# The compact form of the reflections as a stream of its own among the blocks of 16, with other clocks in the planner

## The chip, the cores and the metric

The kernel runs on one core of a Trainium2 chip. The metric is the time of one execution on the device, in microseconds (us); lower is better.

## What is computed

Two layers of a graph network on `x` of 64 x 256 x 256 with one 256 x 256 adjacency matrix `adj`, all in fp32:

```python
# layer 0
h = relu(layernorm(x));  G = adj * adj
h = relu(G @ (h @ W1)); h = relu(G @ (h @ W2)); x = x + G @ (h @ W3)
# layer 1
h = relu(layernorm(x))
deg = sum(adj, 0) + sum(adj, 1) - diag(adj); d = rsqrt(deg)
_, U = eigh(d[:, None] * (diag(deg) - adj) * d[None, :])
h = relu((U.T @ h) @ W1 + b1)
x = x + U @ (h @ W2 + b2)
```

Layer 0 is many matrix products (TensorE). The eigenvectors `U` are one long chain of small, dependent steps, most of them on VectorE. Layer 1 needs both.

## The kernel before, in words

**The chain** (class `Eigen`). `tridiagonalize` (line 393) brings the 256 x 256 matrix to tridiagonal form in 254 steps. In step k, a row `xr` and a column `xc` hold the row and column to be cleared. ScalarE squares and sums the row into `tail` (line 431), VectorE forms `xa` (437), `nn` (440), then through a square root on ScalarE `nb` (450) and `ac` (453). TensorE turns `ac` into a row (`pu`, tile psB, line 454); from it VectorE makes `uau` (465), `c` (467), the row `wr` (469) and the next row `xn` (474, 475), and then, off the shortest way to the next step, the next column (478, 479) and the two updates of the matrix per half (482, 483). The matrix is held as two halves of 128 rows; the first 127 steps work on both, the others on one. The rows get shorter with k: 256 - (k + 1) columns. The vectors of the reflections are kept in `us` (tile q2) and their factors in `gams` (tile z2).

`leaves` (861) then solves 16 blocks of 16 at once. Its core, `all_parts` (721), is 32 sweeps; in each, 15 pairs of a reciprocal and a scalar_tensor_tensor on one column follow one another, and the turning of the vectors of the sweep before lies between them. Its work space is tile q1. At its end it turns its results into matrix form through TensorE (psB, psC) and makes `dc`, the column of eigenvalues. Then `reflections` (502) makes one 256 x 256 matrix `QT` of all 254 reflections: two products of `us`, seven doubling steps (two mask products on VectorE, two products on TensorE, a copy on ScalarE, four products, two subtractions on VectorE from PSUM tile psD), and closing products. `level` (1182) runs for 32, 64, 128 and 256 and merges pairs of blocks; its first TensorE work is to turn `dc` and `zc` into rows (line 1235). `QT` is needed only behind the last level, for `u` and `ut`. After that a flag is computed and read, and a branch (`mend`, 1625) is passed.

**The streams** (class `Layers`). Layer 0 goes over 32 pairs of matrices. `products` (1743) and `rows` (1769) are generators that yield one operation at a time: matrix products with their copies out of PSUM, and norms with loads and stores. `last` adds the result to `x` on VectorE (128x512 from PSUM), `norm1`, `turn_rows` and `for_layer1` make `hw`, the rows that layer 1 begins with. `layer1` (1963) follows when streams and chain are done.

**The order of work.** TensorE and ScalarE execute in exactly the order in which the program issues; VectorE, GpSimd and SyncE are ordered by the compiler's scheduler. `Pace` (143) decides how chain and streams interleave: it keeps a clock for each engine and a time for each tile's content, from costs in `Op` (80): `busy`, for which an engine is taken, and `until`, when a result can be used. Before each chain operation on TensorE it issues stream operations that by its clocks can start before the chain's is ready plus `LATER`; it does so before operations of other engines too. Chain costs are multiplied by `SLOWER`, in the blocks by `IN_BLOCKS`. VectorE's clock may lag behind a waiting operation by `WINDOW` (1.0 us), for the scheduler's freedom. All these operations are recorded on line 188 (`issue`), so that the profile tells them apart by tiles. The costs and the factor of the tie between them are:

```python
    each = 6.3 if self.name == "reciprocal" else 2.0 if self.name == "tensor_tensor_scan" else 1.0
    self.busy = 0.065 + each * n / 960 + 0.08 * sums
    self.until = self.busy + (0.18 if self.name == "scalar_tensor_tensor" else 0.13)
...
    start = max(start, clock[engine])
    clock[engine] = max(clock[engine] + busy, start + busy - self.WINDOW)
```

For TensorE, `busy` is 0.165 for a transpose and the larger of 0.22 and 4 x columns / 2400 for a product.

Of the kernel before, what the change touches and what calls it, by code (L numbers as in the profile page):

```python
# [23 lines left out]
OP = mybir.AluOpType  # L24
# [3 lines left out]
N = 256  # L28
P = 128
H = 2  # L30
# [49 lines left out]
class Op:  # L80


    def __init__(self, part, call, args, kwargs):
        self.engine, self.call, self.args, self.kwargs = ENGINES[part], call, args, kwargs
        self.name = call.__name__
        free = lambda a: int(np.prod([int(n) for n in a.shape[1:]]))
        named = dict(kwargs)
        outs = [named.pop("out")] if "out" in named else [args[0]]
        ins = [a for a in [*(args if "out" in kwargs else args[1:]), *named.values()] if isinstance(a, bass.AP)]
        total = named.pop("accum_out", None)  # L90
        if isinstance(total, bass.AP):
            outs.append(total)
            ins = [a for a in ins if a is not total]
        self.outs, self.ins = [span(a) for a in outs], [span(a) for a in ins]
        n = max(free(a) for a in outs[:1] + ins) if self.engine == "DVE" else free(outs[0])
        sums = len(outs) > 1

        if self.engine == "PE":
            self.busy = 0.165 if "transpose" in self.name else max(4 * n / 2400, 0.22)
            self.until = self.busy + 0.35  # L100
        elif self.engine == "ACT":
            pointers = any(isinstance(kwargs.get(k), bass.AP) for k in ("scale", "bias"))
            self.busy = 0.13 + n / 1400 + 0.12 * pointers + 0.19 * sums
            self.until = self.busy + 0.12
        elif self.engine == "DVE":
            each = 6.3 if self.name == "reciprocal" else 2.0 if self.name == "tensor_tensor_scan" else 1.0
            self.busy = 0.065 + each * n / 960 + 0.08 * sums
            self.until = self.busy + (0.18 if self.name == "scalar_tensor_tensor" else 0.13)
        elif self.engine == "POOL":
            self.busy = 0.2 + 2 * n / 960  # L110
            self.until = self.busy + 0.1
        else:
            self.busy, self.until = 0.1, 4.0


def span(a):

    step = a.ap[0][0]
    lo = a.offset % step if step else a.offset
    return a.tensor.name, lo, lo + sum((int(n) - 1) * abs(int(s)) for s, n in a.ap[1:]) + 1  # L120
# [22 lines left out]
class Pace:  # L143
# [2 lines left out]


    WINDOW = 1.0
    SLOWER, IN_BLOCKS = 1.025, 1.07
    LATER = {"PE": 0.15, "ACT": 0.1}  # L150

    def __init__(self, nc):
        self.slower = self.SLOWER
# [36 lines left out]
    def chain(self, op):  # L190
        if not self.on:
            return op.call(*op.args, **op.kwargs)
        late = self.LATER.get(op.engine, 0.0)
        self.run(self.ready(op) + late, "ACT" if op.engine == "ACT" else None)
        return self.issue(op, self.slower)

    def run(self, limit, whole=None):

        while True:
            first, stream = limit, None  # L200
            for x in self.streams * 2:
                op = x.head()
                if op is not None:
                    start = max(self.ready(op), self.clock[op.engine]) + op.busy * (op.engine == whole)
                    if start < first:
                        first, stream = start, x
            if stream is None:
                return
            self.issue(stream.op)
            stream.op = None  # L210

    def finish(self):
        self.run(float("inf"))
        assert not any(x.more for x in self.streams)
        self.streams, self.on = (), False
# [21 lines left out]
class Eigen:  # L237
# [264 lines left out]
    def reflections(self, us, gams):  # L502


        nc = self.nc
        half = lambda tag: self.mat(tag).rearrange("p h n -> p (h n)")[:, 0 : H * P].rearrange("p (h n) -> p h n", h=H)
        tri = self.mat("m1").rearrange("p h n -> p (h n)")
        tri2 = self.mat("m2").rearrange("p h n -> p (h n)")
        steps = 7
        mask = [(tri if i < 4 else tri2)[:, i % 4 * P : (i % 4 + 1) * P] for i in range(steps)]  # L510
        for i in range(steps):
            nc.sync.dma_start(out=mask[i], in_=self.ap["c_tri"][i])
        s = self.mat("m3")
        self.product(s, us, us, "psD")
        vt = self.mat("m4")
        self.copy_out(vt, self.transpose(us, "psC"))
        t, tt, low, x = half("bs"), half("rb"), half("mask"), half("notm")
        for h in range(H):
            self.tt(t[:, h, :], self.ident[:, 0, 0:P], gams[:, h * P : (h + 1) * P], OP.mult)
        nc.scalar.copy(tt, t)  # L520
        flat2 = lambda v: v.rearrange("p h n -> p (h n)")
        for i in range(steps):
            for h in range(H):
                self.tt(low[:, h, :], s[:, h, h * P : (h + 1) * P], mask[i], OP.mult)
            ps = self.psum("psD")
            for h in range(H):
                at = slice(h * P, (h + 1) * P)
                nc.tensor.matmul(ps[:, at], lhsT=low[:, h, :], rhs=t[:, h, :], start=True, stop=True)
            nc.scalar.copy(flat2(x), ps[:, 0:N])
            ps = self.psum("psD")  # L530
            for h in range(H):
                at, to = slice(h * P, (h + 1) * P), slice(N + h * P, N + (h + 1) * P)
                nc.tensor.matmul(ps[:, at], lhsT=tt[:, h, :], rhs=x[:, h, :], start=True, stop=True)
                nc.tensor.matmul(ps[:, to], lhsT=x[:, h, :], rhs=tt[:, h, :], start=True, stop=True)
            self.tt(flat2(t), flat2(t), ps[:, 0:N], OP.subtract)
            self.tt(flat2(tt), flat2(tt), ps[:, N : 2 * N], OP.subtract)

        g = self.mat("q1")
        ps = self.psum("psD")
        for h in range(H):  # L540
            nc.tensor.matmul(ps[:, h * N : (h + 1) * N], lhsT=t[:, h, :], rhs=vt[:, h, :], start=True, stop=True)
        self.copy_out(g, ps)
        ps = self.psum("psD")
        nc.tensor.matmul(ps[:, 0:N], lhsT=s[:, 0, P:N], rhs=g[:, 0, :], start=True, stop=True)
        nc.scalar.copy(low.rearrange("p h n -> p (h n)"), ps[:, 0:N])
        ps = self.psum("psD")
        nc.tensor.matmul(
            ps[:, 0:N], lhsT=t[:, 1, :], rhs=low.rearrange("p h n -> p (h n)"), start=True, stop=True
        )
        self.tt(g[:, 1, :], g[:, 1, :], ps[:, 0:N], OP.subtract)  # L550
        qt = self.mat("QT")
        ps = self.psum("psD")
        for m in range(H):
            for h in range(H):
                nc.tensor.matmul(
                    ps[:, m * N : (m + 1) * N],
                    lhsT=vt[:, h, m * P : (m + 1) * P],
                    rhs=g[:, h, :],
                    start=h == 0,
                    stop=h == H - 1,  # L560
                )
        self.tt(
            qt.rearrange("p h n -> p (h n)"), self.ident.rearrange("p h n -> p (h n)"), ps, OP.subtract
        )
        return qt


    def scale_and_cut(self, d, e):
# [1041 lines left out]
    def join(self, u, ut, bad, reflections=None):  # L1610
        d = self.row("DV")
        self.nc.vector.tensor_copy(d, self.d)
        self.pace.slower = self.pace.IN_BLOCKS
        zt, dc = self.leaves(d, self.e, bad)
        self.pace.slower = self.pace.SLOWER
        if reflections is not None:
            self.qt = self.reflections(*reflections)
        for n in LEVELS:
            dc = self.level(n, zt, dc, self.rho, self.sg, bad)
        z = self.mat("m0")  # L1620
        self.copy_out(z, self.transpose(zt))
        self.product(u, self.qt, z)
        self.product(ut, z, self.qt)
# [422 lines left out]
```

## Time and profile before

| what | before |
|---|---|
| median of 3 runs (lowest to highest) | 2575.08 us (2575.02 to 2576.18) |
| the profiled execution's own time | 2575.78 us |
| its span, first to last instruction | 2573.6 us |
| mean granted clock of TensorE | 0.991 |
| tridiagonalization, two halves / one half | 22.9 to 836 / 836 to 1467 us |
| blocks of 16 | 1467 to 1893 us |
| reflections | 1893 to 1938 us |
| levels, u and ut | 1938 to 2397 us |
| layer 1 | 2403 to 2574 us |

The first page gives each engine's busy time and the span in 40 slices, a digit for each slice's busy tenths. PE is TensorE's products, PEld its weight loads, DVE VectorE, ACT ScalarE, POOL GpSimd, SP SyncE. An fp32 product shows as two records, and the ends of TensorE's records are modelled, so that a busy TensorE isn't at its peak; start to start is the safer reading. A row of waits names who waited, for whom, the sum in us, how often, and the longest. A row of the timeline gives start, length, engine, line, operation, tiles (out<-in, buffer numbers left out: `m` stands for tiles m0 to m4, `q` for q1 and q2), shape and count, and in brackets the idle time of the engine before it with what ended it. The chain of waits follows the end of the execution back through what released each step.

### The profile page before, as it was taken

What the parts mean: (1) busy time and instruction counts of PE and PEld (TensorE: products, weight loads), DVE (VectorE), ACT (ScalarE), POOL (GpSimd) and SP (SyncE); (2) the same over time, 40 slices, a digit from 0 to 9 for tenths busy, and PEclk for the clock granted to TensorE, in tenths of its full rate; (3) what the DMA queues carried; (4) which work ended last, traced back from release to release, by engine and by line L of the source; (5) the groups of instructions that cost most, each with busy time, mean ns of one, the idle gap of its engine ahead of it and who ended that gap; (6) DMA issues with size and microseconds to landing.
All of it is one profiled execution on the core that took longest, in us unless ns stands there. A gap on an engine that the chain in (4) does not pass through costs nothing. (4 is left out here: it accounts for less than half of the span.)

```text
span 2573.6 us, 38875 instructions
## 1 busy us (share of the span) xinstructions
PE 2414.5 (94%) x8986; PEld 1554.1 (60%) x8986; DVE 2237.4 (87%) x13785; ACT 1027.5 (40%) x3080; POOL 469.7 (18%) x2006
## 2 busy tenths in 40 slices
PE   7888888888899999999999999999999999999899
PEld 3555455545555566666666666565666666565788
DVE  8999999999999999999999999999958898788343
ACT  4234433443344444444444443333433344343322
POOL 1222222222222222223322100000000000000343
PEclk9999999999999999999999999999999999999899
DMA  3000000000000000000000000000000000000576
GB/s 114 17 5 21 17 21 5 21 17 21 5 21 18 21 22 21 22 21 22 22 15 12 22 21 22 21 21 17 21 21 25 9 21 21 21 21 1 171 252 208
DMA packets 59406, 90.06 MB, mean 35 GB/s; under 512 B 5793, under 2 KB 42785, under 8 KB 59169
## 3 DMA queue, kind: packets, MB, share of 16 engines
q1 hardware_dynamic: 59168, 87.52, 10.2%
q8 instruction: 73, 1.20, 0.2%
q14 instruction: 165, 1.34, 0.2%
HBM read 47.13 MB, written 40.37 MB: 34 GB/s over the span
## 5 line engine op out<-in xcount | busy, mean ns | idle before, releaser
L188 PE MATMUL bank<-y,L_gnn_W 128*128 128x512 f32 x2048 | 908.2, 595 | 0.0
L188 PEld LDWEIGHTS bank<-y,L_gnn_W 128*128 128x128 f32 x2048 | 381.3, 191 | 432.3 <-issue 415.1
L188 PE MATMUL bank<-L_gnn_W,s 128*128 128x256 f32 x2048 | 463.8, 380 | 2.5 <-ACT s L188 2.5
L188 PEld LDWEIGHTS bank<-L_gnn_W,s 128*128 128x128 f32 x2048 | 383.4, 191 | 52.9 <-ACT s L188 3.7
L188 ACT ACTIVATE s<-bank 128x512 f32<-128x512 f32 x384 | 223.1, 585 | 153.0 <-PE bank L188 152.2
L188 PE MATMUL bank<-gt,s 128*128 128x256 f32 x1024 | 236.4, 384 | 6.5 <-ACT s L188 6.4
L188 PE MATMUL bank<-L_gnn_W,y 128*128 128x512 f32 x512 | 229.2, 593 | 2.1 <-ACT p L188 2.1
L188 PEld LDWEIGHTS bank<-gt,s 128*128 128x128 f32 x1024 | 193.3, 193 | 42.3 <-ACT s L188 10.3
L188 ACT ACTIVATE junk<-xr 128x254 f32<-128x254 f32 (+63 forms) x254 | 78.0, 307 | 339.6 <-DVE xr L188 333.7
L188 POOL COPY alpha<-xr 128x1 f32<-128x1 f32 x254 | 97.0, 382 | 556.7 <-DVE xr L188 539.1
L1936 POOL TENSOR_TENSOR xb<-x,ub 128x512 f32<-128x512 f32 x64 | 79.8, 1270 | 590.0 <-DVE ub L1902 517.0
L188 PE MATMUL psB<-ident,ac 128*128 128x128 f32 x381 | 86.7, 282 | 105.1 <-DVE ac L188 100.5
L188 ACT COPY y<-bank 128x512 f32<-128x512 f32 x192 | 110.9, 582 | 150.6 <-PE bank L188 150.2
L188 PEld LDWEIGHTS psB<-ident,ac 128*128 128x128 f32 x381 | 42.1, 136 | 212.1 <-issue 148.2
L188 ACT ACTIVATE h<-x,shift,scale 128x256 f32<-128x256 f32 x256 | 136.5, 589 | 66.9 <-DVE shift L188 65.0
L188 PEld LDWEIGHTS bank<-L_gnn_W,y 128*128 128x128 f32 x512 | 95.2, 190 | 101.2 <-issue 89.0
L188 ACT ACTIVATE junk<-x 128x256 f32<-128x256 f32 x256 | 105.6, 412 | 90.0 <-DVE x L188 74.8
L188 ACT ACTIVATE junk<-x,nm 128x256 f32<-128x256 f32 x256 | 129.0, 504 | 27.8 <-DVE nm L188 23.6
L188 DVE SCALAR_TENSOR_TENSOR A<-wr,uc,A 128x255 f32<-128x255 f32 (+63 forms) x381 | 139.6, 367 | 0.0
L188 POOL TENSOR_TENSOR e<-nb,alpha 128x1 f32<-128x1 f32 x254 | 48.1, 189 | 458.7 <-DVE nb L188 449.9
L188 DVE SCALAR_TENSOR_TENSOR q<-q 128x1 f32<-128x1 f32 (+1 forms) x576 | 120.1, 209 | 11.9 <-ACT q L188 1.0
L188 DVE SCALAR_TENSOR_TENSOR A<-xr,wc,A 128x255 f32<-128x255 f32 (+63 forms) x381 | 129.4, 364 | 0.0
(597 smaller groups left out, 4472.2 us busy)
## 6 DMA issues: line engine op xcount, KB each, us to landing
x<-x SPq DMA_DIRECT2D x60, 512.0 KB, 3.4
x<-in_x_dram SPq DMA_DIRECT2D x64, 256.0 KB, 3.6
out_dram<-out SPq DMA_DIRECT2D x64, 256.0 KB, 2.2
hw<-hw SPq DMA_DIRECT2D x60, 256.0 KB, 2.7
L_gnn_W<-in_L_gnn_W_dram SPq DMA_DIRECT2D x1, 2048.0 KB, 11.0
L_gnn_W<-in_L_gnn_W_dram SPq DMA_DIRECT2D x1, 1024.0 KB, 13.6
L_gnn_W<-in_L_gnn_W_dram SPq DMA_DIRECT2D x1, 512.0 KB, 6.4
mask<-in_c_blk_dram SPq DMA_DIRECT2D x2, 256.0 KB, 2.8
```

Of the source, the lines that this page charges most:

```text
L188: return op.call(*op.args, **op.kwargs)
L1936: nc.gpsimd.tensor_tensor(xb[:, :, b, :], x1[:, :, b, :], self.ub2, OP.add)
```

## The change

`reflections` becomes a generator: each instruction that it issued is yielded instead, with the same shapes and in the same order. `join` wraps it in a `Stream`, puts it ahead of the two of layer 0 while `leaves` runs, and issues whatever is left of it by the new `Pace.complete` before the first level. Its matrix `g` goes from tile q1, which `all_parts` uses, to q2. The costs of VectorE in `Op` get a term of 0.06 us for scalar_tensor_tensor and for operations with an operand of one column; the extra time until a result can be used is 0.125 us for all. `SLOWER`, `IN_BLOCKS` and `LATER` for TensorE get other values.

```diff
@@ Op
-            self.busy = 0.065 + each * n / 960 + 0.08 * sums
-            self.until = self.busy + (0.18 if self.name == "scalar_tensor_tensor" else 0.13)
+            pointers = self.name == "scalar_tensor_tensor" or any(a.shape[1:] == [1] for a in ins[1:])
+            self.busy = 0.065 + 0.06 * pointers + each * n / 960 + 0.08 * sums
+            self.until = self.busy + 0.125
@@ Pace
-    SLOWER, IN_BLOCKS = 1.025, 1.07
-    LATER = {"PE": 0.15, "ACT": 0.1}
+    SLOWER, IN_BLOCKS = 1.03, 1.11
+    LATER = {"PE": 0.1, "ACT": 0.1}
+    def complete(self, stream):
+        while stream.more:
+            if stream.head() is not None:
+                self.issue(stream.op)
+                stream.op = None
@@ reflections
-        nc = self.nc
+        nc = self.pace.later
-            nc.sync.dma_start(out=mask[i], in_=self.ap["c_tri"][i])
+            yield nc.sync.dma_start(out=mask[i], in_=self.ap["c_tri"][i])
...
-                self.tt(low[:, h, :], s[:, h, h * P : (h + 1) * P], mask[i], OP.mult)
+                yield nc.vector.tensor_tensor(low[:, h, :], s[:, h, h * P : (h + 1) * P], mask[i], OP.mult)
...
-            self.tt(flat2(t), flat2(t), ps[:, 0:N], OP.subtract)
-            self.tt(flat2(tt), flat2(tt), ps[:, N : 2 * N], OP.subtract)
-        g = self.mat("q1")
+            yield nc.vector.tensor_tensor(flat2(t), flat2(t), ps[:, 0:N], OP.subtract)
+            yield nc.vector.tensor_tensor(flat2(tt), flat2(tt), ps[:, N : 2 * N], OP.subtract)
+        g = self.mat("q2")
...
-        qt = self.mat("QT")
+        self.qt = qt = self.mat("QT")
...
-        return qt
@@ join
         self.pace.slower = self.pace.IN_BLOCKS
+        if reflections is not None:
+            reflections = Stream(self.reflections(*reflections))
+            self.pace.streams = reflections, *self.pace.streams
         zt, dc = self.leaves(d, self.e, bad)
+        if reflections is not None:
+            self.pace.complete(reflections)
         self.pace.slower = self.pace.SLOWER
-        if reflections is not None:
-            self.qt = self.reflections(*reflections)
         for n in LEVELS:
```

More of the change, by code (lines that the diff above doesn't have):

```diff
@@ L511, in reflections @@
         for i in range(steps):
-            nc.sync.dma_start(out=mask[i], in_=self.ap["c_tri"][i])
+            yield nc.sync.dma_start(out=mask[i], in_=self.ap["c_tri"][i])
         s = self.mat("m3")
-        self.product(s, us, us, "psD")
-        vt = self.mat("m4")
-        self.copy_out(vt, self.transpose(us, "psC"))
+        flat2 = lambda v: v.rearrange("p h n -> p (h n)")
+        ps = self.psum("psD")
+        for m in range(H):
+            for h in range(H):
+                yield nc.tensor.matmul(
+                    ps[:, m * N : (m + 1) * N],
+                    lhsT=us[:, h, m * P : (m + 1) * P],
+                    rhs=us[:, h, :],
+                    start=h == 0,
+                    stop=h == H - 1,
+                )
+        yield nc.scalar.copy(flat2(s), ps)
+        vt = self.mat("m4")
+        ps = self.psum("psC")
+        for a in range(H):
+            for b in range(H):
+                yield nc.tensor.transpose(
+                    ps[:, a * N + b * P : a * N + (b + 1) * P],
+                    us[:, b, a * P : (a + 1) * P],
+                    self.ident[:, 0, 0:P],
+                )
+        yield nc.scalar.copy(flat2(vt), ps)
         t, tt, low, x = half("bs"), half("rb"), half("mask"), half("notm")
         for h in range(H):
-            self.tt(t[:, h, :], self.ident[:, 0, 0:P], gams[:, h * P : (h + 1) * P], OP.mult)
-        nc.scalar.copy(tt, t)
-        flat2 = lambda v: v.rearrange("p h n -> p (h n)")
+            yield nc.vector.tensor_tensor(t[:, h, :], self.ident[:, 0, 0:P], gams[:, h * P : (h + 1) * P], OP.mult)
+        yield nc.scalar.copy(tt, t)
         for i in range(steps):
             for h in range(H):
-                self.tt(low[:, h, :], s[:, h, h * P : (h + 1) * P], mask[i], OP.mult)
+                yield nc.vector.tensor_tensor(low[:, h, :], s[:, h, h * P : (h + 1) * P], mask[i], OP.mult)
             ps = self.psum("psD")
@@ L527, in reflections @@
                 at = slice(h * P, (h + 1) * P)
-                nc.tensor.matmul(ps[:, at], lhsT=low[:, h, :], rhs=t[:, h, :], start=True, stop=True)
-            nc.scalar.copy(flat2(x), ps[:, 0:N])
+                yield nc.tensor.matmul(ps[:, at], lhsT=low[:, h, :], rhs=t[:, h, :], start=True, stop=True)
+            yield nc.scalar.copy(flat2(x), ps[:, 0:N])
             ps = self.psum("psD")
@@ L532, in reflections @@
                 at, to = slice(h * P, (h + 1) * P), slice(N + h * P, N + (h + 1) * P)
-                nc.tensor.matmul(ps[:, at], lhsT=tt[:, h, :], rhs=x[:, h, :], start=True, stop=True)
-                nc.tensor.matmul(ps[:, to], lhsT=x[:, h, :], rhs=tt[:, h, :], start=True, stop=True)
-            self.tt(flat2(t), flat2(t), ps[:, 0:N], OP.subtract)
-            self.tt(flat2(tt), flat2(tt), ps[:, N : 2 * N], OP.subtract)
-        g = self.mat("q1")
+                yield nc.tensor.matmul(ps[:, at], lhsT=tt[:, h, :], rhs=x[:, h, :], start=True, stop=True)
+                yield nc.tensor.matmul(ps[:, to], lhsT=x[:, h, :], rhs=tt[:, h, :], start=True, stop=True)
+            yield nc.vector.tensor_tensor(flat2(t), flat2(t), ps[:, 0:N], OP.subtract)
+            yield nc.vector.tensor_tensor(flat2(tt), flat2(tt), ps[:, N : 2 * N], OP.subtract)
+        g = self.mat("q2")
         ps = self.psum("psD")
         for h in range(H):
-            nc.tensor.matmul(ps[:, h * N : (h + 1) * N], lhsT=t[:, h, :], rhs=vt[:, h, :], start=True, stop=True)
-        self.copy_out(g, ps)
+            yield nc.tensor.matmul(ps[:, h * N : (h + 1) * N], lhsT=t[:, h, :], rhs=vt[:, h, :], start=True, stop=True)
+        yield nc.scalar.copy(flat2(g), ps)
         ps = self.psum("psD")
-        nc.tensor.matmul(ps[:, 0:N], lhsT=s[:, 0, P:N], rhs=g[:, 0, :], start=True, stop=True)
-        nc.scalar.copy(low.rearrange("p h n -> p (h n)"), ps[:, 0:N])
+        yield nc.tensor.matmul(ps[:, 0:N], lhsT=s[:, 0, P:N], rhs=g[:, 0, :], start=True, stop=True)
+        yield nc.scalar.copy(low.rearrange("p h n -> p (h n)"), ps[:, 0:N])
         ps = self.psum("psD")
-        nc.tensor.matmul(
+        yield nc.tensor.matmul(
             ps[:, 0:N], lhsT=t[:, 1, :], rhs=low.rearrange("p h n -> p (h n)"), start=True, stop=True
         )
-        self.tt(g[:, 1, :], g[:, 1, :], ps[:, 0:N], OP.subtract)
-        qt = self.mat("QT")
+        yield nc.vector.tensor_tensor(g[:, 1, :], g[:, 1, :], ps[:, 0:N], OP.subtract)
+        self.qt = qt = self.mat("QT")
         ps = self.psum("psD")
@@ L554, in reflections @@
             for h in range(H):
-                nc.tensor.matmul(
+                yield nc.tensor.matmul(
                     ps[:, m * N : (m + 1) * N],
@@ L561, in reflections @@
                 )
-        self.tt(
+        yield nc.vector.tensor_tensor(
             qt.rearrange("p h n -> p (h n)"), self.ident.rearrange("p h n -> p (h n)"), ps, OP.subtract
         )
-        return qt
     def scale_and_cut(self, d, e):
```

## The prediction

> **What bounds the kernel now.** I read the totals and slices of the page, then stretches, waits, the rows around the moved step, and last the chain of waits.
>
> ```profile
> PE 2414.5 (94%) x8986; PEld 1554.1 (60%) x8986; DVE 2237.4 (87%) x13785; ACT 1027.5 (40%) x3080; POOL 469.7 (18%) x2006
> ...
> PE   7888888888899999999999999999999999999899
> ...
> DVE  8999999999999999999999999999958898788343
> ```
>
> Two engines look full. The stretches are tridiagonalization with two row halves, with one half, blocks of 16, reflections, levels, layer 1 (columns: stretch, length, busy time and count of PE, PEld, DVE, ACT, POOL):
>
> ```profile
> 22.90:836.00 813.10, 713.69 (x2670) 435.89 (x2669) 778.97 (x4508) 316.93 (x997) 200.32 (x868) 0.99 0.05 16
> 836.00:1466.70 630.70, 625.04 (x2328) 395.41 (x2328) 586.21 (x4209) 294.25 (x974) 180.62 (x1032) 1.00 0.06 20
> 1466.70:1893.20 426.50, 407.47 (x1380) 252.46 (x1379) 391.32 (x3038) 161.99 (x465) 7.18 (x33) 0.98 0.06 19
> 1893.20:1937.80 44.60, 44.52 (x193) 29.37 (x193) 14.81 (x53) 21.49 (x62) 0.00 (x0) 1.00 0.10 30
> 1937.80:2397.40 459.60, 445.78 (x1613) 287.01 (x1612) 385.90 (x1806) 180.55 (x484) 0.00 (x0) 0.98 0.05 16
> 2403.40:2573.60 170.20, 166.16 (x768) 145.74 (x768) 66.96 (x99) 38.89 (x64) 79.85 (x64) 1.00 0.72 238
> ```
>
> TensorE idles 99 us in the first stretch, 19 in the blocks, 14 in the levels, hardly elsewhere. VectorE is at 92 to 96% until the blocks end and at 33% (14.8 of 44.6 us) in the reflections. The first idle time has one owner, the transposes of line 454, of 0.55 to 0.96 us in the mean per step:
>
> ```profile
> PE psB L188 <- DVE ac L188: 100.5, 126, 2.6
> ```
>
> There the eigen chain sets the pace and TensorE comes too early. The reflections stand alone in the chain (start, length, row, wait before it):
>
> ```profile
> 1894.44 0.08 DVE L188 DVE_READ_ACCUMULATOR junk<-DV,ident 128x1 f32 x1
> 1897.10 0.49 DVE L188 TENSOR_TENSOR mask<-m,m 128x128 f32<-128x128 f32 x2 [2.58 <-ACT m L188]
> ...
> 1934.54 0.42 DVE L188 TENSOR_TENSOR q<-q,psD 128x256 f32<-128x256 f32 x1 [6.13 <-PE psD L188]
> 1937.13 0.69 DVE L188 TENSOR_TENSOR QT<-ident,psD 128x512 f32<-128x512 f32 x1 [2.16 <-PE psD L188]
> 1938.82 0.42 DVE L188 TENSOR_REDUCE tol<-d 128x8 f32<-128x256 f32 x1 [1.01 <-ACT d L188]
> ```
>
> The column that level 32 needs is there at 1894.52; its transposes start at 1937.78, behind the reflections in TensorE's order. Layer 1 needs both streams' and chain's end:
>
> ```profile
> 2399.76 0.59 ACT h L188
> ...
> 2400.40 2.33 PE bank L188 x16
> ...
> 2402.75 0.59 ACT hw L188
> ...
> 2403.39 166.18 PE bank L1688 x768
> ```
>
> So today they end nearly together: the chain's last product at 2397.4 and its flag at 2398.6, the streams' tail at 2403.3, though their last big products ended at 2379.0. The profiled execution took 2575.8 us (2.2 outside its span), 0.7 above the median of 2575.1.
>
> **What the Trainium skill says.** "TensorE: Matmul & The Clock Gate", Architectural detail (its note on queue depths): ScalarE and VectorE take instructions strictly in order. The trace agrees: a chain operation waited 4.09 us on its square root behind a stream's copies. Its Part 1 says that TensorE falls to half clock after an idle window of some 3.4 us and needs as much busy time to be freed; the trace agrees: 0.50 granted between 2386 and 2396, and a 128x256 product took 631 ns where 380 is usual. "VectorE: DVE Perf Modes", errata table: a fixed 58 cycles (120 from PSUM) and one per element at 0.96 GHz, an estimate of 0.19 us for 128 columns and 0.39 for 256 from PSUM. In the trace the second mask product starts about 0.2 after the first, the second subtraction 0.34; I use these.
>
> **The change: the move.** Level 32's transposes come forward from 1937.78 to just after 1894.52. They now wait for a stream product already begun, half of 0.85, and 0.1 of the planner's margin: 43.3 - 0.5 = **-42.8**.
> What moves costs elsewhere. TensorE's 15 us (42 products of 128 columns at 0.22, 12 of 256 at 0.43, four transposes) and ScalarE's copies take stream time, not the chain's; TensorE needn't finish first (below). VectorE: 14 mask products and two starts at 0.2, 15 results from PSUM at 0.34, one of 512 at 0.6: 3.2 + 5.1 + 0.6 = **+8.9**. Bounds: 5, if half fits between dependent steps, and 11.6, their full durations. The nearest rows support a full charge for wide rows: a block step takes 12.1 us bare, 13.6 with ten stream operations, two of them 512 wide.
> New waits: all 32 operations stand in VectorE's order, 16 behind a PSUM result, and the next block step stands behind each. The streams' 64 additions from PSUM waited 2.1 us in all, ScalarE's results about 17: at 0.1 each **+3**, bounds 0 and 14; a gain is excluded since nothing is taken away. The seven 64 KB mask loads go to SyncE before the streams' next issues, landing in 2.4 us: 0, since the streams load ahead. g goes to q2, whose vectors are by then used; `complete` finds nothing left (some 50 us of work in 426).
>
> **The clocks.** They are code, so they move work, not time. First, what they count. A shape is a tuple (load_weights writes `list(t.shape)`), so `a.shape[1:] == [1]` is never true: only scalar_tensor_tensor gets 0.06. Its `until` goes from 0.245 to 0.25 plus elements, others' from 0.195 to 0.19, so dependent paths keep their length.
> In a step with two halves, nine such operations lie from the last row update (line 475) to nn (line 440). On 215 columns they and one product sum to 2.38 before, 2.92 now; times the factors and less WINDOW, nn comes 1.44 after that update before, 2.01 now, while ScalarE's sum allows 1.21. So the planned step grows by 0.57, less 0.05 of LATER: +0.52. Below about 175 columns ScalarE set the old time; at 135 only +0.29 is left. Thus 80 x 0.52 + 47 x 0.38 = **60 us of stream work fills the idle 99**. At 215 columns (steps 32 to 47) the real step is 6.76 with 1.00 of it idle on TensorE, so the planned one is 5.76 and becomes 6.3. With one half, the clock (0.44) is behind ScalarE (1.04): no change but -0.03.
> Price: some steps have less slack than they now lose (a quarter of the waits were under 0.55 for steps 64 to 95, under 0.19 for 96 to 126): about 0.04 in 96 steps and 0.1 in 31, **+3** us (0 to 10). In the blocks 1.11/1.07 lengthens the plan by 3.7%, 15 us, filling about 10 of 19 idle; the chain grows by the 12 above, so neither overtakes the other. Second half and levels: 0, between -5 (margin) and +6 (more counted).
>
> **The end.** The streams' last big products end at 2379 - 60 - 10 = 2309, their tail by 2325; the chain at about 2370. It alone ends. That takes the tail away (layer 1 came 4.8 after the flag, and branches 1.1 after it): **-3.6**. But TensorE is little used for 55 us, so layer 1 starts at half clock: an estimate from the page named, half of 3.4 to 6.8 us lost, **+2.5** (0 to 3.5). The streams' VectorE work that no longer lies in the last level now lies in earlier steps: 0.
>
> Sum: -42.8 + 8.9 + 3 + 3 - 3.6 + 2.5 = -29.0. 2575.8 - 29 = **2547 us**.
>
> **The rivals.** *Blocks take it back*: VectorE, in order, is held at the 32 operations, 0.6 more each: 2567. For it: the reflections' own waits of 2.3 to 2.5 us on psD. Against: in the blocks the sequence lets other work pass, and stream operations hardly wait there.
> *Streams become the end*: the fill fails, their products end at 2369 and 14.5 us of norm, transposes and products follow: layer 1 at 2383.5, not 2403.4, 2556. For it: the balance today. Against: nine counted operations per step.
> *Slower*: TensorE late in every step of the tridiagonalization. It has 0.04 us of slack per step in the second half. Were the shape test to act, nn, nb and c would lengthen that path by 0.18 (127 steps, 23 us), and in the first half seven counts of 0.06 would put the plan at or past the real step, 0.2 x 127 = 25: -29 + 48, 2595. It decides from a mean lateness of 29/254 = 0.11 us.
> *It doesn't act*: reflections stay at the end in VectorE's order: 2576.
>
> **Numbers.** Forecast 0.58 (2533 to 2560), blocks 0.18, streams 0.10, slower 0.06, better than 2531 0.05, no effect 0.03. From 2531 to 2570 leaves out 0.05 below and about 0.14 above. A measurement here can tell 0.2% (5 us) from no change: faster 0.86, same 0.08, slower 0.06.
>
> **What would show it.** Right: waits of psB on ac fall from 100 to about 40 us; blocks last 435 to 442 us; level 32 begins 2 us after them; TensorE's last slices before layer 1 empty for 50 us; layer 1 follows the chain, not hw. Wrong: steps of the tridiagonalization longer than now, VectorE waiting for psD in the blocks, or TensorE full up to layer 1.

## The result and the profile after

The median fell from 2575.63 us (the runs of before beside it) to **2546.72 us**, a ratio of 0.9887 with a 95% interval of 0.987 to 0.9905; 2547 was predicted. The profiled execution's span went from 2573.6 to 2546.6 us, 27.0 less.

The stretches after, in the columns used before (two halves, one half, blocks of 16, levels, layer 1; the reflections have none of their own any more):

```profile
24.00:849.40 825.40, 782.08 (x2944) 483.45 (x2942) 797.35 (x4626) 347.59 (x1073) 204.61 (x887) 1.00 0.05 17
849.40:1461.20 611.80, 606.30 (x2238) 378.79 (x2238) 570.38 (x4109) 290.90 (x961) 176.72 (x1012) 1.00 0.06 20
1461.20:1903.00 441.80, 426.36 (x1522) 271.05 (x1521) 398.95 (x3067) 169.75 (x477) 7.29 (x33) 0.99 0.06 20
1903.00:2368.20 465.20, 419.72 (x1502) 267.96 (x1501) 385.53 (x1810) 175.78 (x474) 0.00 (x0) 0.94 0.05 15
2373.50:2546.60 173.10, 169.05 (x768) 147.96 (x768) 67.41 (x99) 38.92 (x64) 79.62 (x64) 0.98 0.72 234
```

The steps on two halves ended, with the start of step 127, at 849.4 in the change and at 852.0 before, not at 836 as the stretches of before have it. TensorE's idle time in the first stretch is 43 us instead of 99 (100 if read up to 852.0), and it now idles 45 us in the levels, at their end. The wait that owned the first:

```profile
PE psB L189 <- DVE ac L189: 43.9, 89, 1.7
```

VectorE's rows at the move (start, length, row, wait before it): the reflections' work lies between steps of the blocks, without any wait for psD, and is done at 1505; level 32 follows the blocks' end at once:

```profile
1469.56 0.17 DVE L189 TENSOR_TENSOR v<-first,end 128x16 f32<-128x16 f32 x1
1469.65 0.41 DVE L189 TENSOR_TENSOR bs<-bs,psD 128x256 f32<-128x256 f32 x1
1469.98 0.17 DVE L189 SCALAR_TENSOR_TENSOR v<-iota,v 128x16 f32<-128x16 f32 x1
1470.07 0.41 DVE L189 TENSOR_TENSOR rb<-rb,psD 128x256 f32<-128x256 f32 x1
...
1504.36 0.68 DVE L189 TENSOR_TENSOR QT<-ident,psD 128x512 f32<-128x512 f32 x1
...
1904.29 0.08 DVE L189 DVE_READ_ACCUMULATOR junk<-DV,ident 128x1 f32 x1
1907.19 0.42 DVE L189 TENSOR_REDUCE tol<-d 128x8 f32<-128x256 f32 x1 [2.82 <-ACT d L189]
```

TensorE near the end: the last addition's products end at 2306.4, and what follows are the streams' transposes and projections (`eye`, `L_gnn_W`), then the chain's products alone, with waits of 10 and 16 us between:

```profile
2302.68 3.68 PE L189 MATMUL bank<-p,gt 128*128 128x512 f32 x8
2318.06 0.47 PE L189 MATMUL bank<-eye,h 128*128 128x128 f32 x1 [11.70 <-ACT h L189]
...
2321.47 3.79 PE L189 MATMUL bank<-L_gnn_W,h 128*128 128x128 f32 x16 [0.52 <-ACT h L189]
2340.84 1.30 PE L189 MATMUL psB<-ident,m 128*128 128x128 f32 x4 [15.58 <-DVE m L189]
2351.79 3.78 PE L189 MATMUL psA<-q,m 128*128 128x256 f32 x8 [9.65 <-DVE m L189]
...
2373.49 6.75 PE L1715 MATMUL bank<-hw,u 128*128 128x256 f32 x16 [5.03 <-DVEq L1655]
```

The last row says what layer 1 waits for: no longer the streams' `hw`, but the branch behind the chain (L1655 is `tc.If` in `mend`; DVEq is VectorE's sequencer). Stage by stage, in us, from the two traces (the row of level 32 ends where ScalarE copies its rows):

| term | predicted | measured | from |
|---|---|---|---|
| tridiagonalization's end | +3 | -5.5 | 1466.67 to 1461.15 |
| blocks | +11.9 | +15.4 | 426.5 to 441.9 |
| level 32 after the blocks | -42.8 | -41.5 | 45.3 to 3.8 |
| levels, u, ut | 0 | +2.5 | 458.9 to 461.4 |
| chain's end to layer 1 | -3.6 | -0.8 | 6.0 to 5.2 |
| layer 1 | +2.5 | +2.9 | 170.2 to 173.1 |
| sum | -29.0 | -27.0 | span |

### The profile page after: what moved, and what is told of

Same layout as the page of the kernel before. It is cut to its first block, busy times and chain, and to the rows that moved or that the text cites. A ratio compares the mean times of both kernels' runs of the same rounds, so it can differ in the third digit from the quotient of the medians.

```text
span 2546.6 us, 38875 instructions
## 1 busy us (share of the span) xinstructions
PE 2411.5 (95%) x8986; PEld 1554.2 (61%) x8986; DVE 2232.4 (88%) x13785; ACT 1034.7 (41%) x3080; POOL 469.9 (18%) x2006
## 5 line engine op out<-in xcount | busy, mean ns | idle before, releaser
L189 PEld LDWEIGHTS bank<-y,L_gnn_W 128*128 128x128 f32 x2048 | 380.5, 190 | 437.1 <-issue 420.4
L189 PEld LDWEIGHTS bank<-L_gnn_W,s 128*128 128x128 f32 x2048 | 381.4, 190 | 53.2 <-ACT s L189 5.0
L189 PEld LDWEIGHTS bank<-gt,s 128*128 128x128 f32 x1024 | 193.1, 192 | 40.9 <-issue 11.3
L189 PE MATMUL psB<-ident,ac 128*128 128x128 f32 x381 | 86.4, 281 | 48.5 <-DVE ac L189 43.9
## 6 DMA issues: line engine op xcount, KB each, us to landing
L_gnn_W<-in_L_gnn_W_dram SPq DMA_DIRECT2D x1, 2048.0 KB, 10.8
```

## The experiments

The theory: the execution ends when two things have ended, the **chain** and the **streams** with TensorE's idle time; before, both ended at about 2400. The move shortens the chain, the clocks take idle time from the streams, and only both together show. The rival: one of the two parts brings it all.

### Each part alone

`move_only` is the change with these lines as before; `clocks_only` is the kernel before with them as after:

```diff
-            pointers = self.name == "scalar_tensor_tensor" or any(a.shape[1:] == [1] for a in ins[1:])
-            self.busy = 0.065 + 0.06 * pointers + each * n / 960 + 0.08 * sums
-            self.until = self.busy + 0.125
+            self.busy = 0.065 + each * n / 960 + 0.08 * sums
+            self.until = self.busy + (0.18 if self.name == "scalar_tensor_tensor" else 0.13)
...
-    SLOWER, IN_BLOCKS = 1.03, 1.11
-    LATER = {"PE": 0.1, "ACT": 0.1}
+    SLOWER, IN_BLOCKS = 1.025, 1.07
+    LATER = {"PE": 0.15, "ACT": 0.1}
```

> The reflections among the blocks, with every cost and factor of the planner as before. My theory: the chain gets shorter by the move alone; its last product ends 25 to 35 us earlier than the 2397.4 of before, since the tridiagonalization keeps its 1467 us and the blocks grow by 9 to 15. TensorE waits about 100 us for ac again, so the streams' last big products end about 2369 and their tail near 2383, behind or beside the chain: 2552 to 2560 us. Rival (the gain is the clocks'): hardly faster than 2575. If I find 2545 to 2549, the clocks are worth nothing to the time.

> The reflections behind the blocks as before, with the new costs and factors. My theory: the idle time of TensorE before ac falls from 100 to about 44 us and the streams end some 70 us before the chain, but the chain still holds 43 us of reflections: its last product ends within 10 us of 2397.4, and the time lies between 2568 and 2580 us. Rival (TensorE's idle time was the loss): 2520 to 2550.

Measured: the move alone 2578.45 us, ratio 1.0005 (0.9998 to 1.0012), no gain at all: the rival's number, and 18 us above my own range. So it is the clocks alone that speak against the rival: 2569.74, ratio 0.9977 (0.9969 to 0.9986), within my range and far above the 2520 to 2550 of the rival. The profiles give the two ends:

| | chain's last product ends | streams' tail (hw) ends | layer 1 begins |
|---|---|---|---|
| before | 2397.4 | 2403.3 | 2403.4 |
| move alone | 2350.1 | 2405.7 | 2405.7 |
| clocks alone | 2392.2 | 2324.7 | 2397.3 |
| the change | 2368.2 | 2325.9 | 2373.5 |

The move alone shortens the chain by 47 us, more than the 25 to 35 expected and more than in the change, and layer 1 doesn't notice. The chain of waits that ends in layer 1 holds, from the last addition (2385.87) through the norm of the last pair, not one piece of the eigen chain:

```profile
2385.87 0.69 DVE x L188
...
2397.25 1.59 ACT h L188 x3
...
2398.88 1.62 PE bank L188 x6
...
2401.22 3.86 PE bank L188 x16
...
2405.10 0.59 ACT hw L188
...
2405.74 168.04 PE bank L1714 x768
```

And the idle time of TensorE stays with the move alone (first line), while the clocks alone fill it (second):

```profile
PE psB L188 <- DVE ac L188: 100.3, 125, 2.6
...
PE psB L189 <- DVE ac L189: 44.8, 91, 1.7
```

The clocks alone free the streams 79 us earlier and leave the chain behind. The theory of two ends holds; that one part brings it all falls: alone the parts bring nothing and 0.2%, together 1.1%.

### The first 127 steps alone

If that is so, filling the idle time where it is, and nowhere else, should do better than new clocks for all. On top of the move alone:

```diff
         for k in range(N - 2):
             lo = k + 1
+            self.pace.slower = 1.13 if k < 96 else 1.08 if k < 127 else self.pace.SLOWER
```

> The move alone with the costs and factors of before, but with the chain's factor at 1.13 in the first 96 steps of the tridiagonalization and 1.08 in the next 31, which puts some 59 us more stream work there and nowhere else. My theory (two ends: the chain, and the streams with TensorE's idle time; the move shortens the first, the fill the second): waits of psB on ac fall from 100 to 40 to 50 us, the streams' last big products end 50 to 60 us before the 2383 of the move alone, the chain keeps its 2350, give or take 6, and the time is 2526 to 2538, less than the change. Rival (only the new costs, which count the row operations rightly, bring it, or the chain loses in the first half what the streams gain): 2547 or more.

> As the kernel with the fill in the first 127 steps alone, and LATER for TensorE at 0.1 as in the change. If the smaller margin is what made the tridiagonalization 6 us shorter, another 4 to 6 us less than that kernel, 2521 to 2533; if not, the same within 2 us.

Measured: 2530.37 us (0.9823, 0.981 to 0.9836) and, with LATER at 0.1, **2526.75 us** (0.9806, 0.9792 to 0.9819), both faster than the change. The second is 3.6 us under the first, a little less than the 4 to 6 expected of the margin. In it the waits on ac are 55.7 us (53.2 in the first, for 40 to 50 expected), the streams' tail ends at 2350.8 beside the chain's last product at 2347.9, and layer 1 begins at 2353.8. The new costs of the change aren't needed for the gain; a factor in the right place is enough. Of the 20.7 us by which the second's span is shorter than the change's, 9.5 lie in the blocks and 8.8 in the levels with u and ut.

### What the clocks cost the chain

The blocks grew by 15.4 us in the change, by 5.9 with the move alone (426.5 to 432.4), and by 6.3 with the clocks alone (432.8), where no reflections stand among them. In the change VectorE's busy time in them went from 391.3 to 399.0, its idle time from 35.2 to 42.9, and of that its waits for ScalarE from 3.0 to 10.1. The wait that grew most, for the blocks' square roots in q, before and in the change:

```profile
DVE q L188 <- ACT q L188: 1.0, 1, 1.0
...
DVE q L189 <- ACT q L189: 6.9, 6, 2.0
```

In neither does VectorE wait for psD. The one factor, in the change (in the best kernel, the second with the fill, it goes the other way, from 1.07 to 1.11):

```diff
-    SLOWER, IN_BLOCKS = 1.03, 1.11
+    SLOWER, IN_BLOCKS = 1.03, 1.07
```

> The change with IN_BLOCKS at 1.07 again, all else kept. The blocks grew by 15.4 us. Theory A: about 9 of it is the VectorE work of the reflections and the rest comes from ScalarE reaching the square roots late, because the longer plan puts more stream work before them: with 1.07 VectorE's waits for ScalarE's q in the blocks fall from 6.9 to 1 to 3 us, the blocks last 434 to 438 us, and the time is 2540 to 2544. Theory B: it is all the reflections' doing: blocks of 440 to 443 us, 2545 to 2549.

> The kernel with the fill in the first 127 steps and the smaller margin, with IN_BLOCKS at 1.11 in place of 1.07. There the blocks lasted 432.3 us and the time was 2526.8. If the factor is what makes the blocks of the change longer than the move alone does (more stream work before the square roots), they last 436 to 442 us here, with VectorE's waits for ScalarE's q at 5 to 8 us in place of 2.5, and the time is 2530 to 2537. If the factor isn't it, 431 to 434 us and 2525 to 2529.

The change at 1.07: blocks of 437.0, q waits of 3.3 us, but 2547.1 us: the 4.9 us that the blocks gained, the levels lost again, 3.4 of it in the last (149.1 us from its rows to the last product, 145.7 in the change). Its streams ended at 2341 and not 2326, and VectorE's waits for the square roots in `rdq` in that level, 8.4 us for 6.6, make up 1.8 of the 3.4. So theory A had the blocks right, the q waits nearly, and the time wrong. The best kernel at 1.11 in place of 1.07: blocks of 437.4 in place of 432.3, q waits of 4.3 in place of 2.5 (5 to 8 were expected), 2531.37 us (0.9833, 0.982 to 0.9847) in place of 2526.75. There the time rises by 4.6 us, some 6 if each is measured from its own runs of before. Both pairs speak for the factor, but its 5 us in the blocks are little more than what LATER alone does: the first kernel with the fill, also at 1.07, had blocks of 436.0, 3.7 more than the second.

> The change with LATER for TensorE at 0.15 again, all else kept. The tridiagonalization of the change ended 5.5 us earlier than before, where the prediction had 3 us later. Theory A: the smaller margin did it, since TensorE has no idle time with one half and each step waits for it: 0.05 us in 254 steps, at most 12, so the blocks start at 1465 to 1468 us instead of 1461, time 2550 to 2554. Theory B: the fuller first half did it (less streams' work left beside the later steps): the start stays at 1460 to 1462, time 2545 to 2549.

The edit is `0.1` to `0.15` for PE. The blocks began at 1464.4 instead of 1461.2 (before: 1466.7), close to theory A, so the margin is 3.3 of the 5.5; from the first to the second of the kernels with the fill it is 3.0 as well. By halves it is less even. From step 127 to the end the larger margin cost 6.7 us (621.2 in place of 614.5), near to 0.05 in each of 127 steps, but step 127 came 3.5 us earlier, and no run says why; in the pair with the fill, the smaller margin gained 1.6 us there and 1.4 ahead of it. And the time was 2541.36 us, 5 less than the change and below both theories: the blocks took 437.1 us, q waits 3.0, and the levels 4.9 less. Where the chain's square roots fall among the streams' copies shifts with edits of the order; the runs show some 5 us of such shifts and don't say why this edit shifts them so.

One loss in the levels can be read directly. With the streams done, TensorE stood idle between the chain's last products, the granted clock was 0.50, and a group of eight took 3.78 us in the change (first line). With the move alone the streams' products ran in between, the clock was 1.00, and it took 1.97 (second line):

```profile
2364.46 3.78 PE L189 MATMUL psA<-QT,m 128*128 128x256 f32 x8 [0.68 <-ACT u L189]
...
2348.10 1.97 PE L188 MATMUL psA<-QT,m 128*128 128x256 f32 x8
```

The last three such groups together took 10.8 us before, 11.3 in the change, 5.8 with the move alone and 8.8 in the best kernel. With the clocks alone, where the streams were done 68 us before the chain, they took 9.2. So in these runs streams that were done well before the chain cost it some of what the move gave.

### The price of the reflections on VectorE

```diff
-        for i in range(steps):
+        for i in range(1):
```

> The kernel with the fill in the first 127 steps and the smaller margin, with one doubling step of the seven: six are left out, so that the reflections' matrix isn't made whole. They hold 24 of the 32 VectorE operations of the reflections, 6.5 us of the 8.9 that the prediction charged to the blocks. If a wide operation costs the chain its whole share, the blocks last 425 to 427 us in place of 432.3 and the time is 2519 to 2522; if VectorE fits much of it between dependent steps, 428 to 431 us and 2522 to 2526.

Measured: blocks of 432.8 us, against 432.3 with all seven; 2532.13 us; both lie above both guesses. VectorE was busy 3.8 us less and idle 4.2 us more, 1.8 of that in waits for ScalarE. So taking out 24 of the 32 operations gained the blocks nothing, where the full charge would have been 6.5 us. That speaks against the full charge, but other edits of the order moved the blocks by 4 to 5 us, so a cost of a few us could hide behind such a shift. The time, 5 us more, comes from elsewhere: the last level took 146.7 us, against 143.4. Of these 3.3 us, 2.4 are its last three groups of products (11.2 us, against 8.8); here the streams were done 11 us before the chain, in the best kernel 3 us after it.

### The test for one column, made to act

```diff
-            pointers = self.name == "scalar_tensor_tensor" or any(a.shape[1:] == [1] for a in ins[1:])
+            pointers = self.name == "scalar_tensor_tensor" or any(tuple(a.shape[1:]) == (1,) for a in ins[1:])
```

> The change with its test for an operand of one column written so that it acts (tuple against tuple). By the prediction's rival on the slower side the planned step then reaches or passes the real one: TensorE late in both halves of the tridiagonalization, its end some 48 us later than the 1461 of the change, the time about 2595 us. If lateness of TensorE costs less than the sum, because VectorE has other work to do meanwhile, 2550 to 2575; and if the tridiagonalization's end doesn't move, the planner's clocks don't bear on the chain at all.

Measured: 2566.59 us, 0.9964 (0.9952 to 0.9977): 20 us slower than the change, still faster than before, and in the range for lateness that costs less than its sum. The order of the program differs from the change's, so in the change the test doesn't act. The blocks begin at 1486.1, 25 us later than in the change: 19 of them come in the stretch with one row half, where TensorE has hardly any idle time (steps 127 to 253 take 623.3 us instead of 604.0), and 5.5 in the stretch with two (step 127 at 854.9, in the change at 849.4). VectorE's waits for TensorE's row in psB grow from 12.2 to 26.7 us, 14.5 of the 25. The streams are done at 2286.7, and the last level, free of them, takes 135.5 us.

### The branch

> The change without the fallback that a flag would call in (join a second time, from a branch): that part of the computation is left out; these inputs don't need it. In the change layer 1 starts 4.65 us after the flag, in the kernel before it was 4.8, where I had put that down to the streams' tail. Theory A: it is the branch itself, and layer 1 then starts within 2 us of the last product of the chain: 2541 to 2544. Theory B: something else ends late there (a load, the row sums of u): 2545 to 2549.

The edit takes out `eigen.mend(u, ut)`. Measured: 2539.29 us (0.9855, 0.984 to 0.987), 7.4 less than the change and a little below theory A. Layer 1 begins at 2368.5, 0.7 us after the chain's last product, and takes 170.0 us in place of 173.1:

```profile
2368.52 3.72 PE L1715 MATMUL bank<-hw,u 128*128 128x256 f32 x16 [0.46 <-ACT ut L189]
```

It is the branch: layer 1 starts 5.0 us earlier (2373.5 to 2368.5), and is 3.1 us shorter, nearly all of it in these first 16 products, which took 6.75 us in the change.

## Why the prediction was right, and where it was not

The bound was read rightly: chain and streams end together, and each part of the change frees one. The forecast of the fill held closely: waits on ac of 43.9 us for about 40, the streams' last products at 2306 for 2309, their tail at 2326 for 2325, the chain's end at 2368 for 2370. Level 32 came forward by 41.5 us for 42.8. In the fill there is some luck: the first stretch gave 56.6 of the 60 us forecast, but the blocks 3.6 of the 10. What made up for it was not in the forecast: 4 us less idle time in the levels ahead of the last addition, and 9 us less busy time of the streams' products.

Four terms had other sizes than the sum gave them: the tridiagonalization by -8.5 us, the blocks by +3.5, the chain's end by +2.8 and the levels by +2.5. That they cancel to 2 us in the span, and that the median falls on 2547 itself, is luck.

*"VectorE ... +8.9"* and *"at 0.1 each +3"*, the blocks. The total was near (11.9 for 15.4), the reasons not. With the move alone VectorE's busy time in the blocks grew by 4.9 us (391.3 to 396.2), the forecast's lower bound, taking out 24 of the 32 operations made nothing shorter, and VectorE never waited for psD. What came in their place was ScalarE: 7.1 us more of waits for it in the change, 5.9 of them for q. And the clocks, put at nothing here, lengthened the blocks by 6.3 us without any reflections in them; at 1.11 they were 4.9 and 5.1 us longer than at 1.07. "Neither overtakes the other" was wrong by that.

*"Price: some steps have less slack than they now lose, +3"*: the tridiagonalization ended 5.5 us earlier. The lateness didn't show (step 127 came at 849.4, before at 852.0), and LATER, put at up to -5 with the levels, is worth 3.3. The rest appears, with LATER kept at 0.15, in both kernels with a fuller first half (2.3 and 4.6 us), and its cause was not tried.

*"Second half and levels: 0"*: the levels, with u and ut, took 2.5 us more, 0.5 of it in the last three groups of products. The rest was not traced.

*"That takes the tail away: -3.6"*: 0.8. I read the branch instruction, 1.1 us after the flag, as the end of the branch; VectorE, for which layer 1's first product waits, is let go only 4.6 us after the flag, and 4.3 in the kernel before, with a tail. The kernel without the branch settles that.

*"Streams become the end ... 2556"*: the rival's mechanism is what the move alone runs into, but its number was 22 us too low. I let 10 us of idle time in the blocks be filled, which was to be the new factor's work, and took 14.5 us for the tail; it took 22.5 (2383.2 to 2405.7). The other 4 us are the chain's last products, which now stand ahead of the streams' last ones on TensorE. TensorE's work and idle time being unchanged, so is the time.

*"Slower ... 2595"*: the mechanism is real, its sum of 48 us was 25: 19 from the second half, put at 23, and 5.5 from the first, put at 25. That VectorE has other work in the first half while TensorE is late would explain the difference; no run tests it.

## What to carry to other kernels

When two chains of work end together, a change that shortens one shows nothing, and a change that shortens the other shows little; look for the pair before judging either alone. Find where the shared engine idles, and move work into that place rather than change the planner's costs everywhere: the factor on 127 steps brought 2526.8 us, the costs for all 2546.7. Streams that are done long before the chain aren't free either: TensorE, left idle, ran chain products at half clock at the end. A test in a planner that never acts shows in no profile; compare the order of the program with the test on and off.

## What the runs showed of the hardware

Passing a branch that isn't taken cost 4.6 us from the flag's computation to the first instruction behind it on VectorE, for which TensorE's first product waited (2368.8 to 2373.4), though the compare itself stands 0.6 us after the flag; what fills the time between is not shown. TensorE was already at half the clock at the end of the levels, stood idle for the 5 us of the branch, and then ran layer 1's first 5 us at half the clock too:

```profile
2360.00:2373.00 13.00, 7.78 (x18) 5.68 (x18) 0.31 (x2) 1.17 (x2) 0.00 (x0) 0.50 0.01 3
2373.00:2378.00 5.00, 4.51 (x11) 3.65 (x12) 1.87 (x4) 0.00 (x0) 2.92 (x3) 0.50 0.69 201
2378.00:2383.00 5.00, 5.00 (x21) 4.25 (x20) 0.81 (x2) 1.84 (x3) 5.00 (x5) 0.83 1.00 395
2383.00:2393.00 10.00, 10.00 (x48) 8.81 (x47) 4.09 (x6) 2.43 (x4) 4.40 (x4) 1.00 0.44 150
```

The columns are those of the stretches; the granted clock is the third from the end. Without the branch the chain's last products ran at 0.50 as well, but layer 1 had 1.00 from its start (2368.5 to 2373.5).
